# First chunk of attention's input moved ahead of bias and router work, experts' columns prepared earlier, last division in four pieces

## The chip, the core and the metric

The kernel runs on one core of a Trainium2 chip. The metric is the device time of one execution, in microseconds (us), as a median over several runs. TensorE (PE) does matrix products, VectorE (DVE) elementwise work and reductions, ScalarE (ACT) activations and copies, GpSimd (POOL) elementwise work and indirect transfers, and SyncE (SP) issues transfers. ACT and POOL issue transfers too. Each engine takes its own instructions in the order that was fixed when the program was built.

## The reference, cut to what matters

An image of 256 channels and 64 x 64 points passes through two layers. Layer 0 is a windowed linear attention on the image. Layer 1 takes the 4096 points as tokens of 256 channels: full attention with 8 heads, and then a mixture of 8 experts, of which each token uses two.

```python
x = x + _L0_conv_ref(_gn(x), L0_conv_Wq, L0_conv_Wk, L0_conv_Wv, L0_conv_Wout, L0_conv_bout)
t = _to_tokens(x)
t = t + _L1_attn_ref(_ln_t(t), L1_attn_w_qkv, L1_attn_b_qkv, L1_attn_w_out, L1_attn_b_out)
t = t + _L1_ffn_ref(_ln_t(t), L1_ffn_Wr, L1_ffn_br, L1_ffn_ln_g, L1_ffn_ln_b, L1_ffn_W1, L1_ffn_b1, L1_ffn_W2, L1_ffn_b2)
x = _from_tokens(t, x)
```

In attention, `qkv = x @ w_qkv + b_qkv`, a softmax over `q k^T / 16` for each head, and a projection with `w_out` and `b_out`. In the expert layer, `logits = xt @ Wr + br` choose two experts; each expert normalizes with its own gain and shift (`ln_g`, `ln_b`), multiplies by `W1`, adds `b1`, applies gelu, and multiplies by `W2`.

## The kernel before

All data is float32. The tokens lie as 32 tiles of 128 tokens (`t`, 264 columns: 256 channels and 8 columns for the router's logits). A chunk is four tiles, 512 tokens; there are 8 chunks (`NCH`).

**Layer 0** (to about 1000 us) runs twice, once for each half of the channels: `prepare` makes keys, values, queries and sums, and `attend` does the masked products. Its last sigmoids are those of `by_channel` (L367). `root` (L254) is a one-column tile whose square root serves only to have the table of sqrt loaded on ScalarE early; the square root of the group norm follows it.

**The q, k, v products of layer 1** (L814 to L965). First the transfers are issued: `w_out` on ACT's queue (L821), the QKV weights and the router's weights on SP's (L838, L839), the bias rows and two rows that are broadcast over all partitions on ACT's (L841 to L845). Then come two pieces of small work. The biases of q and k are transposed from six rows into six columns (`bqk`, L847 on TensorE, L849 on VectorE). The router's weights are folded into attention: the sums of their columns and the product with `b_out` (L856 on TensorE, L863 and L865 on VectorE), a transposed copy of `w_out` (L870, L871), and its product with the router's weights (L875, L882), so that the projection gives the logits' columns as well.

Then the loop over chunks. `begin(c)` takes the statistics of the chunk's four tiles (L793, L794 on VectorE), adds epsilon (L798, VectorE) and takes the square root (L799, ScalarE). It is called one chunk ahead. `end` takes the reciprocal (L802). For each tile, VectorE writes the normalized tile `hn` (L898, in two buffers), TensorE transposes it (L808), ScalarE copies it from PSUM to `act` (L809), and GpSimd adds the row of `b_out` to `t` (L908). Then q and k of the chunk are computed channel by channel (L914), and VectorE adds the bias (L918) and takes the largest absolute value (L919). The value products (L925) are evacuated by VectorE (L932), and the logits' part by ScalarE (L933). All these products, transposes included, share four PSUM banks. After the loop, a bound on the scores is computed (L950 to L965), and a branch (L978) on it chooses between two forms of attention; the first is taken, and the code of the other is jumped over at its end.

**Attention** (1120 to about 2287 us): for each chunk of queries and each half of the heads, scores (L1025), exp (L1036), sums of exp on VectorE (L1043) and products with the values (L991). The last sum is divided directly by `divide`: a reciprocal of 128 x 512 elements out of PSUM (L1072) and a product (L1067). Then the last four tiles are projected and added to `t` (L972, L975), with their statistics for the next norm (L793, L794).

**Routing and experts** (from about 2287 us). The experts' biases and norm parameters are loaded as three blocks of rows on ACT's queue (L1237), transposed on TensorE (L1239), copied on VectorE (L1240), and written to memory as one table, `crows` (L1244, ACT's queue), from which each slot of the expert loop later takes its expert's columns (L1216, SP's queue). Behind the first two of these copies on VectorE stand the norm of all tiles (L798, L799, L802) and the routing; it ends in lists by which GpSimd gathers tokens (L1445). The expert loop (L1485, L1494) runs to about 2829 us, and the image is put together at the end.

The order within each engine's queue comes from a planner that places instructions when the program is built, by their order in the source and by the times at which it expects inputs and buffers to be ready. A block under `tc.issue_after(ins)` keeps the instructions in it behind `ins` in the queue of the engine of `ins`.

## Time and profile before

| | us |
|---|---|
| median of 3 runs | 2881.29 (2879.69 to 2881.95) |
| the profiled execution, its own time | 2876.29 |
| its span, first to last instruction | 2874.5 |
| first q, k, v product (L914) starts | 1014.78 |
| first score product of attention (L1025) starts | 1120.05 |
| last division (L1072) starts | 2277.91 |
| norm ahead of routing (L798) starts | 2292.75 |
| first gather of an expert's tokens (L1445) starts | 2332.34 |

The times in the lower rows count from the span's start. In a timeline row, the first number is the start, the second the duration of what is merged in the row (as many instructions as xN says), then engine, line, operation, output<-inputs; in brackets stands how long the engine was idle before it and which work ended that idle time. "issue" there means that the engine waited for nothing that the profile shows. The granted clock is the share of TensorE's full clock.

### The profile page before, as it was taken

To read this page: it belongs to the slowest core of one execution; us is meant where nothing else is said; L and a number is where in the kernel's file an instruction comes from. 1 tells how busy PE (TensorE), PEld (TensorE's weight loads), DVE (VectorE), ACT (ScalarE), POOL (GpSimd) and SP (SyncE) were. 2 spreads that over 40 slices of the span, in tenths; PEclk is the share of its full clock that TensorE was granted. 3 is DMA by queue.
4 is the path that set the end of the run, shared out by engine and by line. 5 is a ranking of instruction groups with operands and counts; after the bars stand their busy time and mean duration, and the time that the engine had idled before them with its cause. 6 is when DMAs were issued, how large, how long until landed. Compare 5 with 4: busy or idle time off the path is not lost.

```text
span 2874.5 us, 73093 instructions
## 1 busy us (share of the span) xinstructions
PE 2722.7 (95%) x31182; PEld 1265.9 (44%) x31182; DVE 2078.1 (72%) x3019; ACT 1504.6 (52%) x2086; POOL 717.9 (25%) x804
## 2 busy tenths in 40 slices
PE   6889999988999999999999999999999779999996
PEld 5454346735434553222222222222222258888884
DVE  6758788575778777999999999999999841111113
ACT  3232423223332314888888888888888643222222
POOL 1067778116777621000000000000000022222220
PEclk9999999999999999999999999999999969999997
DMA  5000000000000000000000000000000056666665
GB/s 140 6 26 28 7 31 13 7 7 24 24 14 27 27 1 1 6 6 6 6 5 6 6 6 6 5 6 6 6 6 6 8 193 205 193 220 196 194 220 187
DMA packets 104212, 149.71 MB, mean 52 GB/s; under 512 B 18338, under 2 KB 79368, under 8 KB 103876
## 3 DMA queue, kind: packets, MB, share of 16 engines
q1 hardware_dynamic: 88984, 118.05, 12.7%
q0 software_dynamic: 6528, 17.83, 2.2%
q10 hardware_dynamic: 8364, 9.02, 0.9%
q8 instruction: 249, 4.08, 0.6%
q14 instruction: 87, 0.71, 0.1%
HBM read 126.76 MB, written 18.12 MB: 50 GB/s over the span
## 4 chain that ended last, share of the span: by engine, by line
PE 57%; DMA 2%; DVE 1%; issue 1%; ACT 0%; SPq 0%; POOL 0%; ACTq 0%; DVEq 0%; POOLq 0%
PE ps_two L1025 20%; PE ps_acc L991 18%; PE ps_hp L1485 8%; PE ps_yp L1494 8%; PE ps_den L972 1%; PE ps_den L991 1%; DMA y<-yrows 1%; PE ps_tp L1460 1%; DMA w<-in_L_ffn_W 0%; PE ps_two L972 0%; DVE t L1537 0%; DMA yrows<-y,target 0%; DVE rec L1072 0%; ACT pe L1036 0%; DVE total L1043 0%
## 5 line engine op out<-in xcount | busy, mean ns | idle before, releaser
L1036 ACT ACTIVATE pe<-ps_two 128x1024 f32<-128x1024 f32 x1024 | 992.4, 1021 | 142.5 <-PE ps_two L1025 127.3
L1043 DVE TENSOR_TENSOR total<-total,pe 128x1024 f32<-128x1024 f32 x928 | 1058.0, 1214 | 0.0
L1025 PE MATMUL ps_two<-qk 32*64 32x512 f32 x8192 | 620.2, 613 | 3.6 <-POOLq L978 1.8
L991 PE MATMUL ps_acc<-pe,v 128*32 128x512 f32 x4096 | 546.4, 605 | 0.2 <-ACT pe L1036 0.2
L561 ACT COPY sm<-ps_sc 128x384 f32<-128x384 f32 (+3 forms) x454 | 218.5, 511 | 523.8 <-PE ps_sc L734 344.3
L565 DVE TENSOR_TENSOR sm<-ps_sc,mask 128x512 f32<-128x512 f32 (+3 forms) x740 | 340.0, 519 | 71.8 <-PE ps_sc L734 68.0
L565 POOL TENSOR_TENSOR sm<-sm,mask 128x192 f32<-128x192 f32 (+3 forms) x428 | 350.1, 847 | 111.9 <-ACT sm L561 111.5
L1025 PEld LDWEIGHTS ps_two<-qk 32*64 32x64 f32 x8192 | 166.5, 129 | 421.0 <-PE ps_two L1025 379.0
L1488 ACT ACTIVATE hid<-ps_hp,cols 128x256 f32<-128x256 f32 (+1 forms) x288 | 133.0, 462 | 360.6 <-PE ps_hp L1485 359.5
L1303 POOL MEMSET on<- 128x256 f32 x1 | 0.3, 311 | 1166.6 <-PE ps_den L991 1166.6
L991 PEld LDWEIGHTS ps_acc<-pe,v 128*32 128x32 f32 x4096 | 80.7, 108 | 416.5 <-issue 402.5
L1485 PE MATMUL ps_hp<-xe,w 128*128 128x256 f32 (+1 forms) x1152 | 246.8, 371 | 0.0
L1494 PE MATMUL ps_yp<-w,hid 128*128 128x256 f32 x1088 | 240.8, 379 | 0.0
L734 PE MATMUL ps_sc<-qk 32*64 32x384 f32 (+3 forms) x3584 | 231.9, 458 | 0.0
L1485 PEld LDWEIGHTS ps_hp<-xe,w 128*128 128x128 f32 x1152 | 201.3, 190 | 39.5 <-ACT hid L1488 5.3
L1494 PEld LDWEIGHTS ps_yp<-w,hid 128*128 128x128 f32 x1088 | 204.2, 190 | 26.4
L750 PE MATMUL ps_acc<-sm,v 128*32 128x256 f32 (+3 forms) x2688 | 213.2, 419 | 0.2
L565 POOL TENSOR_TENSOR sm<-sm,ycut 128x384 f32<-128x384 f32 (+4 forms) x146 | 147.5, 1031 | 250.4 <-ACT sm L561 250.1
L1464 DVE TENSOR_SCALAR xe<-ps_tp,cols 128x256 f32<-128x256 f32 (+1 forms) x72 | 34.8, 525 | 239.6 <-PE ps_tp L1460 217.1
L565 DVE TENSOR_TENSOR sm<-ps_sc,ycut 128x384 f32<-128x384 f32 (+4 forms) x254 | 128.8, 559 | 90.0 <-PE ps_sc L662 88.0
L1496 DVE TENSOR_TENSOR y<-ps_yp,b 128x256 f32<-128x256 f32 x68 | 28.9, 424 | 194.8 <-PE ps_yp L1494 194.7
L734 PEld LDWEIGHTS ps_sc<-qk 32*64 32x64 f32 (+1 forms) x3584 | 108.6, 157 | 111.4 <-DVE sm L565 67.6
(237 smaller groups left out, 2230.6 us busy)
## 6 DMA issues: line engine op xcount, KB each, us to landing
w<-in_L_ffn_W SPq DMA_DIRECT2D x72, 1024.0 KB
by<-recs SPq DMA_DIRECT2D x48, 256.0 KB
b<-in_L_ffn_b SPq DMA_DIRECT2D x36, 128.0 KB
rows<-in_x SPq DMA_DIRECT2D x16, 256.0 KB
zrows<-act SPq DMA_DIRECT2D x4, 1024.0 KB
y<-yrows SPq DMA_DIRECT2D x8, 512.0 KB
y<-yrows ACTq DMA_DIRECT2D x8, 512.0 KB
rec<-recs SPq DMA_DIRECT2D x60, 64.0 KB
```

Of the source, the lines that this page charges most:

```text
L561: nc.scalar.copy(sm[:, :used], sc[:, :used])
L565: done = engine.tensor_mul(to, of, mk.unsqueeze(1).to_broadcast(list(to.shape)))
L734: nc.tensor.matmul(scs[h][u : u + rows, at : at + n], kT[hs[h], P * i + u : P * i + u + rows], qT[hs[h], CH * ix + CELL * c0 : CH * ix + C ...
L750: nc.tensor.matmul(acc[hs[h], CELL * c0 : CELL * c1], v[:, i, hs[h]], sms[h][:, at : at + n], start=not begun[0], stop=last and at == plac ...
L991: nc.tensor.matmul(to[D * hd : D * (hd + 1), :], lhsT(hd), rhs[:, hd, :], start=start, stop=stop, skip_group_check=True,)
L1025: nc.tensor.matmul(sc[hd // 2][CELL * u : CELL * (u + 1), hd % 2, :], qk[hs, 1, g, P * i + CELL * u : P * i + CELL * (u + 1)], qk[hs, 0, g ...
L1036: nc.scalar.activation(pe[:, pair, :], s, AF.Exp, scale=C**-0.5)
L1043: add = nc.vector.tensor_add(to, first[:, pair, :] if i == 1 else to, pe[:, pair, :])
L1464: nc.vector.tensor_scalar(xe[:, k, :n], tp[:, k, :n], cols[:, gain], cols[:, shift], op0=ALU.mult, op1=ALU.add,)
L1485: nc.tensor.matmul(hp[:, :n], w1[:, k, tok(m)], x_now[:, k, :n], start=k == 0, stop=k == KC - 1)
L1488: nc.scalar.activation(hid[:, m, :n], hp[:, :n], AF.Gelu, bias=cols[:, m : m + 1])
L1494: nc.tensor.matmul(yp, hid[:, m, tok(j)], w2[:, m, :], start=m == 0, stop=m == NH - 1)
```

## The change

- **First chunk.** The transposes of the biases and the router's work become two functions, `biases` and `router`. For chunk 0, normalization and transposes come first in the queues of VectorE and TensorE; behind them `biases` and the statistics of chunk 1; `router` follows chunk 0's value products on both engines. `hn` has four buffers.
- **Tables of sqrt.** One more square root of `root` stands behind the last sigmoid of layer 0, and `root` is kept through layer 0 for it; another, of one element, stands at the beginning of routing's code.
- **Experts' columns.** Loads, transposes and copies of the experts' rows move from the beginning of routing into the loop of the q, k, v products, after chunk 2. The copies go to ScalarE, the four transfers to SP's queue.
- **Last division.** Reciprocal and product are done in four pieces of 128 columns, in turn.

```diff
-            root = small.tile([P, 1], F32, name="root")
+            root = wts.tile([P, 1], F32, name="root")
             nc.scalar.sqrt(root, ident[:, :1])
...
+        sigmoid = [None]
...
-                nc.scalar.activation(qk[:, n, CH * i : CH * (i + 2)], pr.rearrange("p j n -> p (j n)"), AF.Sigmoid)
+                sigmoid[0] = nc.scalar.activation(qk[:, n, CH * i : CH * (i + 2)], pr.rearrange("p j n -> p (j n)"), AF.Sigmoid).ins
...
+            if g == KC - 1:
+
+                with tc.issue_after(sigmoid[0]):
+                    nc.scalar.sqrt(root, ident[:, :1])
             with tc.tile_pool(name="c_work", bufs=1) as work, psum("c_ps2", 1) as ps:
                 attend(g, work, ps, *of)
...
-            nc.tensor.transpose(tp[:, tok(k)], src[:, tok(k)], ident)
+            last = nc.tensor.transpose(tp[:, tok(k)], src[:, tok(k)], ident)
         nc.scalar.copy(dst, tp[:, :C].rearrange("p (k n) -> p k n", k=KC))
+        return last
...
+    e_dram = ctx.enter_context(tc.tile_pool(name="e_dram", bufs=1, space=bass.MemoryType.DRAM))
+    crows = e_dram.tile([NE, P, NH + 2 * KC], F32, name="crows")
+
+    def expert_columns(pool, ps):
+        cols = pool.tile([P, NE, NH + 2 * KC], F32, name="cols")
+        at = 0
+        for name, n in (("L1_ffn_b1", NH), ("L1_ffn_ln_g", KC), ("L1_ffn_ln_b", KC)):
+            rw = pool.tile([NE * n, P], F32, name=f"{name}_rows")
+            nc.sync.dma_start(rw, a[name].rearrange("e (k p) -> (e k) p", p=P))
+            tp = ps.tile([P, CH], F32, tag="mm", name="ps_mm")
+            nc.tensor.transpose(tp[:, : NE * n], rw, ident[: NE * n, : NE * n])
+            nc.scalar.copy(cols[:, :, at : at + n], tp[:, : NE * n].rearrange("p (e k) -> p e k", e=NE))
+            at += n
+        nc.sync.dma_start(crows.rearrange("e p n -> p e n"), cols)
...
-            tp = ps.tile([P, CH], F32, tag="mm", name="ps_mm")
-            nc.tensor.transpose(tp[:, :6], rows6, ident[:6, :6])
             bqk = win.tile([P, 6], F32, name="bqk")
-            nc.vector.tensor_copy(bqk, tp[:, :6])
...
-            rp = ps.tile([P, CH], F32, tag="mm", name="ps_mm")
...
+            def biases():
+                tp = ps.tile([P, CH], F32, tag="mm", name="ps_mm")
+                nc.tensor.transpose(tp[:, :6], rows6, ident[:6, :6])
+                nc.vector.tensor_copy(bqk, tp[:, :6])
+
+            def router():
+
+
+                rp = ps.tile([P, CH], F32, tag="mm", name="ps_mm")
+                for n, by in enumerate((lambda k: ones[:, :1], lambda k: bqk[:, 4 + k : 5 + k])):
+                    for k in range(KC):
+                        nc.tensor.matmul(
+                            rp[:, NE * n : NE * (n + 1)],
+                            by(k).to_broadcast([P, P]),
+                            wr[:, k, :],
+                            start=k == 0,
+                            stop=k == KC - 1,
+                        )
+                nc.vector.tensor_copy(wr_sum, rp[:, :NE])
+                nc.vector.tensor_copy(bo_wr, rp[:, NE : 2 * NE])
+                for j in range(KC):
+                    tp = ps.tile([P, CH], F32, tag="mm", name="ps_mm")
+                    for k in range(KC):
+                        nc.tensor.transpose(tp[:, tok(k)], wo[:, k, tok(j)], ident)
+                    nc.vector.tensor_copy(woT[:, j, :], tp[:, :C])
...
                 tp = ps.tile([P, CH], F32, tag="mm", name="ps_mm")
                 for k in range(KC):
+                    for j in range(KC):
+                        nc.tensor.matmul(
...
+                nc.vector.tensor_copy(wo[:, :, C:], tp[:, : KC * NE].rearrange("p (k e) -> p k e", e=NE))
...
             begin(0)
             for c in range(NCH):
-                if c + 1 < NCH:
+                if 0 < c < NCH - 1:
                     begin(c + 1)
                 norm.end(NB * c, NB * (c + 1))
                 for i in range(NB * c, NB * (c + 1)):
-                    hn = work.tile([P, C], F32, name="hn")
-                    nc.vector.tensor_scalar(
+                    hn = work.tile([P, C], F32, name="hn", bufs=4)
+                    last = nc.vector.tensor_scalar(
...
-                    to_channels(hn, act[:, :, tok(i)], ps)
+                    turned = to_channels(hn, act[:, :, tok(i)], ps)
 
                     nc.gpsimd.tensor_add(t[:, i, :C], t[:, i, :C], bo)
+                if c == 0:
+
+                    with tc.issue_after(last.ins), tc.issue_after(turned.ins):
+                        biases()
+                        begin(1)
                 for s in range(2):
...
-                    nc.vector.tensor_add(v[:, i, :], pv[:, :C], bv)
+                    biased = nc.vector.tensor_add(v[:, i, :], pv[:, :C], bv)
                     nc.scalar.copy(t[:, i, C:], pv[:, C : C + NE])
+                if c == 0:
+                    with tc.issue_after(biased.ins), tc.issue_after(product.ins):
+                        router()
+                if c == 2:
+                    expert_columns(win, ps)
...
-                                def divide(den=den, whole=whole, times=times):
+                                def divide(den=den, whole=whole, to=to):
                                     whole()
                                     rec = work.tile([P, CH], F32, tag="rec", name="rec")
-                                    nc.vector.reciprocal(rec, den[0])
-                                    times(rec)
+                                    for n in range(CH // P):
+                                        nc.vector.reciprocal(rec[:, tok(n)], den[0][:, tok(n)])
+                                        nc.vector.tensor_mul(to[:, tok(n)], to[:, tok(n)], rec[:, tok(n)])
...
+
+        root = small.tile([1, 1], F32, name="root")
+        nc.scalar.sqrt(root, ident[:1, :1])
         cst.update(constants_of("m", wts))
...
-        crows = dram.tile([NE, P, NH + 2 * KC], F32, name="crows")
         br = row_on_all("L1_ffn_br", NE, wts)
...
-            cols = r_work.tile([P, NE, NH + 2 * KC], F32, name="cols", bufs=1)
-            at = 0
-            for name, n in (("L1_ffn_b1", NH), ("L1_ffn_ln_g", KC), ("L1_ffn_ln_b", KC)):
-                rw = r_work.tile([NE * n, P], F32, tag="rw", name=f"{name}_rows")
-                nc.scalar.dma_start(rw, a[name].rearrange("e (k p) -> (e k) p", p=P))
-                tp = bank()
-                nc.tensor.transpose(tp[:, : NE * n], rw, ident[: NE * n, : NE * n])
-                nc.vector.tensor_copy(
-                    cols[:, :, at : at + n], tp[:, : NE * n].rearrange("p (e k) -> p e k", e=NE)
-                )
-                at += n
-            nc.scalar.dma_start(crows.rearrange("e p n -> p e n"), cols)
```

The lines of the biases' and router's former place, ahead of the loop, are removed; their text is that of the two functions.

## The prediction

> **What bounds the kernel now.** I read the page first, then the busy time by stretch around the start of layer 1 (about 1000 us), the timeline there, and the timeline at the end of layer 1's attention (2277 to 2296 us). The page gives the frame:

> ```profile
> span 2874.5 us, 73093 instructions
> PE 2722.7 (95%) x31182; PEld 1265.9 (44%) x31182; DVE 2078.1 (72%) x3019; ACT 1504.6 (52%) x2086; POOL 717.9 (25%) x804
> ...
> q8 instruction: 249, 4.08, 0.6%
> q14 instruction: 87, 0.71, 0.1%
> ```

> TensorE is busy 95% of the span, so time can only come out of the few stretches where it waits. The change touches two. The first, with the engines' busy time by stretch (PE, PEld, DVE, ACT, POOL, then granted clock, DMA share, GB/s):

> ```profile
> 1000.00:1007.00 7.00, 0.59 (x3) 0.19 (x1) 4.49 (x17) 1.49 (x2) 0.12 (x1) 0.72 0.64 190
> 1007.00:1015.00 8.00, 7.01 (x30) 5.85 (x31) 5.50 (x26) 1.81 (x6) 2.90 (x4) 0.50 0.00 0
> 1015.00:1028.00 13.00, 13.00 (x33) 6.95 (x34) 9.69 (x31) 0.68 (x5) 1.51 (x2) 0.80 0.00 1
> 1028.00:1041.00 13.00, 11.90 (x42) 6.94 (x41) 12.94 (x46) 2.57 (x12) 3.02 (x4) 1.00 0.01 1
> ...
> 1054.00:1067.00 13.00, 12.05 (x45) 7.08 (x42) 9.31 (x17) 1.91 (x8) 2.98 (x4) 1.00 0.00 0
> ```

> For 6.4 us TensorE does nothing while weights land (190 GB/s, all of it before 1007); then 7 us of small work at half clock; then products, which fill TensorE (12 of 13 us per chunk) until attention starts at 1120. The timeline shows what each engine waited for:

> ```profile
> 1003.38 1.28 ACT L799 ACT_TABLE_LOAD   x1 [8.06 <-DVE ln_mv L794]
> ...
> 1007.26 0.24 PE L847 MATMUL ps_mm<-cst,bias_rows 6*128 6x6 f32 x1 [6.67 <-DMA L_attn_b_out_all<-in_L_attn_b_out]
> ...
> 1007.61 0.17 DVE L849 COPY bqk<-ps_mm 128x6 f32<-128x6 f32 x1 [2.95 <-PE ps_mm L847]
> ...
> 1009.50 0.40 DVE L898 TENSOR_SCALAR hn<-t,ln_mv,ln_rstd 128x256 f32<-128x256 f32 x1
> ...
> 1014.78 9.81 PE L914 MATMUL ps_mm<-act,wqkv 128*128 128x512 f32 x16 [0.46 <-ACT act L809]
> ```

> VectorE's queue is in order: the bias copy (L849) waits, through L847, for the bias rows' DMA until 1007.6 (the row names the last of the DMAs behind it), and the first chunk's normalization (L898), whose statistics were ready by 1003.3, stands behind it. So the first product starts at 1014.78. The second place is the end of attention:

> ```profile
> 2277.91 3.36 DVE L1072 RECIPROCAL rec<-ps_den 128x512 f32<-128x512 f32 x1 [1.15 <-PE ps_den L991]
> 2281.37 0.69 DVE L1067 TENSOR_TENSOR act<-act,rec 128x512 f32<-128x512 f32 x1
> ...
> 2289.93 0.17 DVE L1315 TENSOR_SCALAR steps<-cstm 128x16 f32<-128x16 f32 x1 [2.66 <-issue]
> 2292.52 0.31 DVE L1240 COPY cols<-ps_mm 128x64 f32<-128x64 f32 x2 [2.42 <-issue]
> 2292.75 0.17 DVE L798 TENSOR_SCALAR ln_rstd<-ln_mv 128x32 f32<-128x32 f32 x1
> ```

> Here everything hangs on VectorE: last division, projection's sums, then (after the branch around the other attention) routing, up to the gathers at 2332.

> **First chunk ahead.** Statistics of four tiles end about 1003.1 (chunk 1's no longer mixed in). The sqrt then runs without the 1.28 us table load, at 1003.3; reciprocal 0.17, four normalizations at about 0.37 apart from 1003.7 to 1005.3; eight transposes at half clock (four took 1.09 us) and the ScalarE copies (0.37 each) end about 1006.9. The bias transpose, now behind them on TensorE, still waits for its rows until 1007.2; the QKV weights, on SP's queue, are in by then, since the DMA share is 0.00 after 1007. The first product starts at about 1007.5, not 1014.78: **7.3 us** earlier. Behind the waiting bias copy on VectorE are now chunk 1's statistics (4 x 0.5 us), which are not wanted before 1020. GpSimd's sums L908, now early, wait for the b_out row; only the projection, much later, needs them. The DMA issues on ACT's queue stay where they were and end at 1003.07, before the sqrt.

> The moved router work is not gone. It is 16 small matmul instructions and 4 transposes, 5.0 us before at half clock (1.02 + 1.00 + 1.09 + 1.89), in time when TensorE had nothing else ready. Now it stands between chunk 0's and chunk 1's products at full clock: 16 x 0.215 us (the value products[...] are 3.72/16 = 0.23 apart) + 4 x 0.15 = 4.0 us. A chunk's boundary has 1.0 us of idle TensorE that could hide some, and the waits for VectorE's woT copies may add as much; I take **4.0** (3 to 6).

> [...] The row: the clock read 0.50 from 1004 to 1020, through 7 us of small matmuls, and rose only 5.3 us after the dense products began. [...] by the row the same 5.3 us. I take the row, and ±0.9 us[...].

> **Table loads.** The new sqrt after the last sigmoid of layer 0 costs 1.28 + 0.2 us of ScalarE, hidden by its 17 us without work there (611.5 to 630.4, but for one copy). If placed before that copy, 0.2 us. The second, ahead of routing, replaces a load at 2288.5 that nothing waited for: nothing.

> **Four hn buffers.** With two, each chunk's tiles 2 and 3 are normalized only after the transposes of 0 and 1, and TensorE waits 0.49 and 0.46 us at each boundary. With four, one wait remains (the last value bank's ScalarE copy). About 0.25 us over 6 or 7 boundaries: **1.5** (0 to 3.5).

> **Experts' columns.** Added in chunk 2: three row loads and one store on SP (about 0.4 us of issue each; the store waits there for the copies, and nothing of SP's stands behind it before attention; the loads are 48 KB among 1.3 MB, about 0.15 us of transfer), three transposes (0.2 us each) and three ScalarE copies. They take three PSUM banks out of the rotation of four: **-0.5** (0 to -1.5). Taken away at the end: two VectorE copies ahead of L798, 0.23 us, with their semaphore instructions about **0.3**; four ACT issues, which hid behind VectorE anyway. The third copy lay in a ScalarE wait: nothing.

> **Last division in pieces.** Reciprocals of 128x128 take 0.94 us at L620, from SBUF; a quarter of L1072 is 0.84; I take 0.9. Each piece has a 0.1 us dependency and a product of 0.29 (L1319's shape): 5.2 us instead of 4.15, but the first projection starts after 1.3. VectorE then need not wait: 5.2 plus 3.3 us of sums and statistics end at 2286.4, not 2287.26: **0.9** (0.5 to 1.2).

> **After the branch.** VectorE stands idle 2.66 us, runs one instruction, and stands again (2.42), with no wait on another engine. In this stretch the instruction queue q14 brings two blocks. [...] The row has 0.71 MB in 87 packets, about 8 KB each[...]. The branch target lies just ahead of a block's end, so two fetches are paid. The pieces add at least six instructions ahead of it; the target should slide into the next block, and one fetch falls away. [...] Semaphore instructions can shift it too, so I take most: **1.9** (0 to 2.25).

> **Sum.** 7.3 - 4.0 + 1.5 - 0.5 + 0.3 + 0.9 + 1.9 = 7.4 us. Against the profiled execution: span 2874.5 to 2867.1, its own time 2876.3 to 2868.9. The median of the runs lies 5.0 us above that execution; the same difference gives 2881.3 - 7.4 = **2873.9**. A measurement tells about 0.2% (5.8 us) from no change, so the forecast lies only just outside.

> **Rivals.**
> - *Both fetches stay*: the target is still ahead of a block's end. For it: the semaphore count is unknown. 7.4 - 1.9 = 5.5: 2875.8, within 0.2%. Chance 0.15.
> - *VectorE sets the pace in the first chunks.* It was 12.94 of 13 us busy from 1028 to 1041. A chunk needs 9.35 us of it; with 28 tiles' statistics (14 us) and the router's 1.4 over three chunks that is 43.4 against 38.6: up to 4.8 us lost, 2878.7. Against it: statistics have no haste. Chance 0.10.
> - *It doesn't do what it says*: the products wait for the QKV weights to 1011, which nothing used before 1014. 3.5 us lost, 2877.4. Against: no DMA after 1007. Chance 0.05.
> - *More*: boundaries and router hide fully (+2 and +1): 2870.9. Chance 0.15.
> - *Slower*: the router on TensorE waits for two woT copies in VectorE's full queue, with chunk 1's products queued behind. [...] It must eat 7.4 + 5.8 = 13.2 us, so it decides from two waits of 5.3 us; then 2887. Against: these copies kept TensorE 0.1 us before. Chance 0.05.

> The likeliest has 0.50, its own range 2871.5 to 2876. The bound of 0.2% lies at 2875.5: **faster 0.70** (0.48 of the likeliest, 0.15 of the fourth, about half of the first rival), **same 0.25** (the rest of these two, and the second and third rivals), **slower 0.05**. The range, 2870 to 2879, leaves out the slower case and the tails.

> **What would show it.** First L914 near 1007.5, L799 without a table load, attention at about 1115.8 (1120.05 less 4.3); one idle gap on VectorE after the branch; L798 near 2285.4 (2292.75 less 7.4). Wrong if L914 starts after 1010, if TensorE pauses over 2 us before chunk 1, or if the gap is still double.

## The result and the profile after

In a first series, six runs of each kernel, the changed kernel took 2869.84 us (2867.64 to 2871.2) and the kernel before 2880.08 (2879.19 to 2881.95): ratio 0.9962, 95% interval 0.995 to 0.9975. A second series gave 2863.21 against 2877.4, ratio 0.9954 (0.994 to 0.9967). The change makes the kernel faster by 0.25 to 0.6%. The forecast, 7.4 us or a ratio of 0.9974, lies at the edge of the first interval and outside the second: right in sign, too small by 3 to 7 us. 2869.84 is also 0.16 us below the range's low end.

The head and two queues of the changed kernel's page:

```profile
span 2869.0 us, 73086 instructions
PE 2723.5 (95%) x31182; PEld 1263.6 (44%) x31182; DVE 2079.2 (72%) x3022; ACT 1505.2 (52%) x2091; POOL 718.0 (25%) x804
...
q8 instruction: 249, 4.08, 0.6%
q14 instruction: 87, 0.71, 0.1%
```

Its own time is 2870.81 us. Nothing in the totals tells the story: TensorE's work is the same, and so are the page's two instruction queues (q8, q14). The stretches tell it. The busy time by stretch at the start of layer 1, whose first load is now issued at 1004.04 (before: 1000.63), same columns as before:

```profile
1004.00:1007.00 3.00, 0.01 (x1) 0.00 (x0) 2.61 (x10) 0.18 (x1) 0.12 (x1) 0.96 0.55 112
1007.00:1011.00 4.00, 2.04 (x9) 1.67 (x9) 3.09 (x11) 1.51 (x5) 0.00 (x0) 0.50 0.74 258
1011.00:1016.00 5.00, 5.00 (x7) 2.23 (x8) 4.82 (x18) 0.41 (x2) 4.47 (x7) 0.50 0.01 2
1016.00:1024.50 8.50, 8.50 (x27) 5.09 (x26) 8.06 (x22) 0.50 (x3) 1.30 (x2) 0.94 0.00 1
1024.50:1028.80 4.30, 3.39 (x30) 2.91 (x28) 3.20 (x13) 1.56 (x6) 1.04 (x2) 1.00 0.00 0
1028.80:1041.00 12.20, 11.78 (x40) 6.91 (x40) 12.20 (x40) 2.17 (x10) 2.50 (x4) 1.00 0.01 2
```

The seven microseconds of small work at half clock are gone from the front (row two holds chunk 0's own eight transposes and, at its end, that of the biases). They come back, shorter, in row five, between chunk 0 and chunk 1 at full clock. In the timeline of the same place:

```profile
1006.82 0.20 ACT L805 ACTIVATE ln_rstd<-ln_rstd 128x4 f32<-128x4 f32 x1 [8.08 <-DVE ln_rstd L804]
...
1007.34 1.38 DVE L924 TENSOR_SCALAR hn<-t,ln_mv,ln_rstd 128x256 f32<-128x256 f32 x4
...
1010.90 0.24 PE L875 MATMUL ps_mm<-cst,bias_rows 6*128 6x6 f32 x1 [1.11 <-DMA bias_rows<-in_L_attn_b_out]
...
1011.12 10.01 PE L945 MATMUL ps_mm<-act,wqkv 128*128 128x512 f32 x16
...
1024.53 0.51 PE L884 MATMUL ps_mm<-wqkv,ones 128*128 128x8 f32 x4
...
1024.89 0.59 PE L884 MATMUL ps_mm<-wqkv,bqk 128*128 128x8 f32 x4
...
1025.34 0.64 PE L896 MATMUL ps_mm<-cst,wo 128*128 128x128 f32 x4
...
1026.37 0.36 PE L901 MATMUL ps_mm<-wqkv,woT 128*128 128x8 f32 x2 [0.39 <-DVE woT L897]
...
1027.05 0.73 PE L901 MATMUL ps_mm<-wqkv,woT 128*128 128x8 f32 x6
```

No table load stands before the square root (L805). The four normalizations follow each other (L924). TensorE then waits 1.11 us for the bias rows (L875), and the first product (L945) starts 7.08 us after the first load; it was 14.15. The end of attention, VectorE's timeline:

```profile
2277.06 1.77 DVE L1109 RECIPROCAL rec<-ps_den 128x128 f32<-128x128 f32 x2 [1.18 <-PE ps_den L1027]
2278.75 0.42 DVE L1110 TENSOR_TENSOR act<-act,rec 128x128 f32<-128x128 f32 x2
2279.09 1.76 DVE L1109 RECIPROCAL rec<-ps_den 128x128 f32<-128x128 f32 x2
2280.77 0.42 DVE L1110 TENSOR_TENSOR act<-act,rec 128x128 f32<-128x128 f32 x2
2281.11 0.77 DVE L1011 TENSOR_TENSOR t<-ps_two,t 128x264 f32<-128x264 f32 x2
...
2286.87 0.17 DVE L1340 TENSOR_SCALAR steps<-cstm 128x16 f32<-128x16 f32 x1 [2.66 <-issue]
2286.96 0.17 DVE L804 TENSOR_SCALAR ln_rstd<-ln_mv 128x32 f32<-128x32 f32 x1
...
2289.26 0.43 DVE L1303 TENSOR_TENSOR logit<-logit,L_ffn_br_all 128x256 f32<-128x256 f32 x1 [0.65 <-DVE again L1278]
```

The pieces end when the whole division would have (2281.11 is 4.05 us after its start; before, 3.36 + 0.69), but the projection's sums follow without a pause. After the branch the first idle gap is as long as before (2.66). The second, 2.42 before, has shrunk to 0.65 and moved behind six more instructions.

Single executions differ by several microseconds ahead of layer 1 (its first load is issued anywhere from 998.0 to 1004.4 us in the fourteen profiles of this case), so runs are compared by stretch, each counted from the start of the event that opens it to the start of the one that ends it (last statistics: their end).

| us | before | after | after, again |
|---|---|---|---|
| first load to first product | 14.15 | 7.08 | 6.90 |
| chunk 0, first product to first value product | 9.65 | 9.85 | 9.00 |
| last value product of chunk 0 to chunk 1 | 2.65 | 4.48 | 4.49 |
| the same, chunk 2 to 3 (experts' columns) | 2.51 | 2.62 | 2.62 |
| the same, other chunks | 2.51 to 2.58 | 1.97 | 1.96 |
| first load to start of attention | 119.42 | 111.70 | 110.67 |
| attention to its last division | 1157.86 | 1161.32 | 1157.79 |
| last division to last statistics | 9.36 | 7.15 | 7.15 |
| last statistics to first gather | 45.07 | 43.24 | 43.23 |

The edited stretches gain 7.7 + 2.2 + 1.8 = 11.8 us in the first profile (12.8 in the second). The first span is only 5.5 us shorter because two things went the other way: layer 0 took 3.4 us more, and attention 3.5 more through the clock (last section). Layer 0 has one small edit, the added square root at 614 us; but TensorE's 8000th product there, at about 546 us, was 2.0 us late already, so most of the 3.4 us does not come from it.

### The profile page after: what moved, and what is told of

It is laid out like the page before. It is cut to its first block, busy times and chain, and to the rows that moved or that the text cites. A ratio compares the mean times of both kernels' runs of the same rounds, so it can differ in the third digit from the quotient of the medians.

```text
span 2869.0 us, 73086 instructions
## 1 busy us (share of the span) xinstructions
PE 2723.5 (95%) x31182; PEld 1263.6 (44%) x31182; DVE 2079.2 (72%) x3022; ACT 1505.2 (52%) x2091; POOL 718.0 (25%) x804
## 3 DMA queue, kind: packets, MB, share of 16 engines
q8 instruction: 249, 4.08, 0.6%
## 4 chain that ended last, share of the span: by engine, by line
PE 57%; DMA 1%; DVE 1%; issue 1%; SPq 0%; ACT 0%; POOL 0%; POOLq 0%; DVEq 0%; ACTq 0%
PE ps_two L1061 20%; PE ps_acc L1027 18%; PE ps_hp L1510 8%; PE ps_yp L1519 8%; PE ps_den L1008 1%; PE ps_den L1027 1%; DMA y<-yrows 1%; PE ps_tp L1485 0%; DMA w<-in_L_ffn_W 0%; DVE t L1562 0%; DMA xs<-zrows,source 0%; PE ps_mm L1568 0%; DMA yrows<-y,target 0%; DVE rec L1109 0%; POOL xs L1470 0%
## 5 line engine op out<-in xcount | busy, mean ns | idle before, releaser
L1072 ACT ACTIVATE pe<-ps_two 128x1024 f32<-128x1024 f32 x1024 | 992.6, 1021 | 145.0 <-PE ps_two L1061 130.2
```

Source lines behind the costliest of these rows:

```text
L1072: nc.scalar.activation(pe[:, pair, :], s, AF.Exp, scale=C**-0.5)
```

## The experiments

**Two hn buffers in the changed kernel**

```
-  hn = work.tile([P, C], F32, name="hn", bufs=4)
+  hn = work.tile([P, C], F32, name="hn", bufs=2)
```

> The changed kernel with two hn buffers instead of four. Theory (the buffers take away TensorE's waits at each chunk's boundary): the chunks' products start 12.8 us apart again instead of 12.28, so attention starts 3.2 to 3.8 us later after the first weights' transfer than the changed kernel's 111.7 us. Rival (the closer chunks come from elsewhere, such as the new order of VectorE's queue): still 12.28, attention at 111.7. On the fetch after the branch: the program then has 14 more VectorE instructions ahead of the branch's target, which puts the target behind a block's boundary; theory: one idle gap of about 2.7 us and none of 0.65 after it.

Measured: 2872.76 us (one run; before 2881.27). Between the later chunks TensorE again takes 2.51 us, with the experts' columns 3.12; the seven boundaries together are 4.0 longer than the changed kernel's. Attention starts 115.83 after the first load, 4.1 later; that this agrees is partly chance, since chunk 1 lost 1.7 us to the half clock here, while the first product and chunk 0 were 1.5 quicker. The second gap after the branch is gone. So by the boundaries the buffers are worth 4.0 us. That is more than the 1.5 of the prediction, and above its upper bound of 3.5.

**Four hn buffers in the kernel before, and nothing else**

```
-  hn = work.tile([P, C], F32, name="hn")
+  hn = work.tile([P, C], F32, name="hn", bufs=4)
```

> The kernel before with four hn buffers and nothing else. Theory of the buffers: 12.28 us from chunk to chunk where the kernel before has 12.82, from chunk 1 on, so attention starts about 116.2 us after layer 1's first load instead of 119.4 (3.2 sooner). Theory that the changed kernel's closer chunks came from something else (statistics begun in another order, the router moved): 12.82 stays, and attention starts at 119.4. Theory of the blocks: the branch's target then stands 16 VectorE instructions ahead of the block's end (it was 2), so the first stop after the branch stays at 2.7 to 3.0 us, and the second, 2.13 before, is gone. Median by both theories 5.3 us below the kernel before; by the first alone 3.2.

Measured: 2870.47 us (2868.51 to 2871.51) against 2878.43, ratio 0.9968 (0.9954 to 0.9981): 8.0 us by the medians, where 5.3 were expected. Last statistics to first gather takes 42.97 (2.1 less). Attention starts at 114.51 (expected 116.2), 4.9 sooner than before: 4.0 from the boundaries, the rest in the first product and in chunk 0's clock. So one word of the change brings 4.0 us at the boundaries and, by way of the second gap after the branch (below), 2.1 behind it; the other 0.9 lies in stretches that also vary between profiles of one kernel. A chunk boundary of the kernel before, TensorE's timeline:

```profile
1053.84 0.60 PE L808 MATMUL ps_mm<-cst,hn 128*128 128x128 f32 x4
1054.93 0.73 PE L808 MATMUL ps_mm<-cst,hn 128*128 128x128 f32 x4 [0.49 <-DVE hn L898]
1056.13 7.13 PE L914 MATMUL ps_mm<-act,wqkv 128*128 128x512 f32 x16 [0.46 <-ACT act L809]
```

and one with four buffers:

```profile
1064.89 1.28 PE L808 MATMUL ps_mm<-cst,hn 128*128 128x128 f32 x8
1066.64 1.55 PE L914 MATMUL ps_mm<-act,wqkv 128*128 128x512 f32 x3 [0.46 <-ACT act L809]
```

The wait of 0.49 for tiles 2 and 3 goes whole, and the transposes run 0.05 closer; the wait of 0.46 for ScalarE's copy stays whole. Over the seven boundaries that is 0.68 + 0.60 + 5 x 0.54 = 4.0 us.

**The router's products behind the biases, ahead of chunk 0's own products**

```
   biases()
+  router()
   begin(1)
...
-  if c == 0:
-      with tc.issue_after(biased.ins), tc.issue_after(product.ins):
-          router()
```

> The changed kernel with the router's work right behind the biases, ahead of chunk 0's products. Theory (the work itself is cheap at full clock and partly fits into the boundary's idle time; at half clock it stands alone on TensorE): the first product starts 4 to 5 us later than the changed kernel's 7.1 us after the first transfer, the boundary before chunk 1 shrinks by 2.0 to 2.4 us, and attention starts 2 to 3 us later. Rival (moving the router behind chunk 0 wins nothing, only the order of the first chunk did): attention starts within 0.5 us of the changed kernel's 111.7 us.

Measured: 2868.68 us (one run). First product 10.26 after the first load (3.2 later, expected 4 to 5). The boundary shrinks from 4.48 to 1.97: the router costs **2.51** there, not 4.0. But the first chunk's products took 11.65 (9.85), as the half clock lasted longer, and the boundary with the experts' columns took 0.4 more; attention starts 2.9 later. Without the clock's 1.8, the router's place between the chunks is worth about 1 us; how much of the 1.8 is chance one run can't say.

**The last division whole again**

```
-  for n in range(CH // P):
-      nc.vector.reciprocal(rec[:, tok(n)], den[0][:, tok(n)])
-      nc.vector.tensor_mul(to[:, tok(n)], to[:, tok(n)], rec[:, tok(n)])
+  nc.vector.reciprocal(rec, den[0])
+  nc.vector.tensor_mul(to, to, rec)
```

> The changed kernel with the last reciprocal and product undivided. Theory: from the start of the reciprocal to the last tile's statistics 9.3 us again instead of 7.15, TensorE's projection starting 4.2 us after the reciprocal instead of 2.0. Rival (the pieces gain only because the statistics after them are ordered better): 7.2 to 8. After the branch, 14 VectorE instructions stand ahead of the block's end; they take over 2.3 us, so by the fetch theory there is one gap of about 2.7 us and no second one.

Measured: 2867.9 us (one run). Division to last statistics 9.82, against 7.15 in pieces: 2.7 us. VectorE's timeline shows where:

```profile
2272.17 3.36 DVE L1108 RECIPROCAL rec<-ps_den 128x512 f32<-128x512 f32 x1 [1.18 <-PE ps_den L1027]
2275.98 0.69 DVE L1109 TENSOR_TENSOR act<-act,rec 128x512 f32<-128x512 f32 x1 [0.46 <-DVE rec L1108]
2277.48 0.99 DVE L1011 TENSOR_TENSOR t<-ps_two,t 128x264 f32<-128x264 f32 x2 [0.81 <-PE ps_two L1008]
```

VectorE waits 0.46 for its own reciprocal and 0.81 for the projection; ahead of the last sum it waits another 1.06. In pieces none of these appears. The kernel before didn't have the first of them (its product started 0.10 after the reciprocal's end), so this run overstates the gain: the change itself brought the 2.2 of the table.

**Where the branch's target stands.** Two runs move only the number of VectorE instructions ahead of the target. In the kernel before, and in the changed one:

```
+  junk = wts.tile([P, 1], F32, name="junk")
+  for _ in range(3):    # 6 in the changed kernel
+      nc.vector.memset(junk, 0.0)
```

> The kernel before with three one-element memsets on VectorE at the very beginning, while it waits for the image. Theory (the second gap after the branch is the fetch of the next block of instructions, which ended two instructions behind the branch's target): the target now stands behind the boundary, the gap of 2.4 us ahead of the experts' columns is gone, and the first copy of columns starts within 0.5 us of the first instruction after the branch. Rival (the gap was a wait of the columns' copies for released memory or for another engine): it stays at 2.2 to 2.4 us.

Measured: 2875.59 us (one run; before 2881.27). The second gap is gone, last statistics to first gather 43.15 (45.07): 1.9 us, though the first gap is 0.3 longer here (2.97).

> The changed kernel with six one-element memsets on VectorE at the very beginning, while it waits for the image. This moves the branch's target back to where it stood before the change, two instructions ahead of a block's end. Theory (fetch of the next block): after the branch two instructions run, then a second gap of 2.1 to 2.3 us stands where the changed kernel has 0.6, and routing is 1.5 to 1.7 us later. Rival (the gap of before belonged to the experts' columns, which are gone here): the second gap stays at 0.6 or vanishes.

Measured: 2868.05 us (one run; before 2877.4). The second gap is back, as in the kernel before, and the first gather comes 1.4 us later. VectorE's timeline with six instructions added:

```profile
2282.70 0.17 DVE L1343 TENSOR_SCALAR steps<-cstm 128x16 f32<-128x16 f32 x1 [2.67 <-issue]
2282.78 0.17 DVE L807 TENSOR_SCALAR ln_rstd<-ln_mv 128x32 f32<-128x32 f32 x1
2285.04 0.42 DVE L1303 TENSOR_TENSOR logit<-ln_mv,wr_sum 128x256 f32<-128x256 f32 x1 [2.08 <-issue]
```

The VectorE instructions of each program ahead of the target, counted in the compiled program (a jumped-over form of attention included), against the second gap:

```
program                      ahead   runs before the 2nd gap   2nd gap, us
four buffers, before          7089   -                         none
whole division                7091   -                         none
changed kernel                7097   8                         0.58
router early                  7098   7                         0.76
kernel before; after + 6      7103   2                         2.13; 2.08
kernel before + 3             7106   -                         none
two buffers, after            7111   -                         none
```

One place, behind instruction 7105, fits all of them: with two instructions left to it the second gap is 2.08 to 2.13 us, with seven and eight 0.76 and 0.58, with 14 or 16, or past it, there is none. In the kernel before and in the changed one, single packets of 8 KB start on q14, by the page an instruction queue, at 1.0 and at 3.4 us after the branch. The first stop ends 2.83 us after the branch in both; the second ends 5.14 and 5.15 us after it, whether two instructions ran ahead of it or eight. Each stop ends 1.72 to 1.82 us after the start of one of these packets. That the packets are fetches of the instructions that follow, and that one ends behind 7105, is the author's reading of these times and counts. (The gaps here are from the end of any instruction, semaphores too, so 0.58 for the row's 0.65 and 2.13 for its 2.42.)

**The changed kernel again**, unchanged, five runs.

> The changed kernel unaltered, for its time beside the following kernels and for a second trace. Theory [...]: times fall into groups 3 to 3.5 us apart, and this trace may show the clock either way; the stretches outside such drops repeat to 0.3 us (last division to last statistics 7.15, the second gap after the branch 0.58 to 0.65, chunks 12.28 apart). Rival (the drop belongs to the changed program): the clock reads 0.50 for 8 us after the start of attention here too.

Measured: 2863.21 us (2862.32 to 2866.35) against 2877.4; the table above has its stretches. Every edited stretch repeats within 0.2 us, except chunk 0's products. Attention takes 1157.79, as before the change, so its longer time in the first profile doesn't belong to the changed program as such. Six of the fourteen profiles met a half clock near attention's start, among them one with the old order (three instructions added to the kernel before: 1159.77); how often each kernel meets it, fourteen profiles can't say. The times do fall into two groups, 2862.3 to 2863.2 and 2865.9 to 2866.4, but drops at attention's start don't explain them: the profiled execution is of the upper group and had none.

**A guard against a stop at the start of attention**: the exp's table loaded early, and one filler product behind the bound's.

```
+  early = small.tile([1, 1], F32, name="early")
+  with tc.issue_after(logits.ins):
+      nc.scalar.activation(early, ident[:1, :1], AF.Exp)
...
+  fill = ps.tile([P, CH], F32, tag="mm", name="ps_mm")
+  with tc.issue_after(bounding.ins):
+      for k in range(KC):
+          nc.tensor.matmul(fill, wqkv[:, k, tok(0)], act[:, k, chunk(0)], ...)
```

> The changed kernel with two things at the start of attention: a one-element exp on ScalarE behind the last copy of the logits, so that exp's table is loaded during the branch, and one more product (4 matmul instructions, 1.7 us, into a bank that nobody reads) behind the bound, so that TensorE doesn't pause. Theory [...]: the first exp runs 1.3 us sooner after the first score products, the clock stays at 1.00, and the median is 1.3 us plus some part of 3.4 us below the changed kernel's, 1.5 to 4 us. Rival [...]: 1.3 us or less.

Measured: 2862.39 us (2861.11 to 2865.12), ratio 0.9951 (0.9937 to 0.9965), not to be told from the changed kernel's 2863.21. In the profiled execution, attention to division took 1156.53, 1.3 less, at full clock; but chunk 1 ran a while at half clock (its dense products 8.67 us, not 6.97), which took 1.7 back.

**The early table alone** (the edit above without the filler)

> The changed kernel with a one-element exp behind the last of the logits' copies, so that the exp's table is loaded while TensorE still works on the last products. Theory that attention's first step waits for the table: start of attention to last division 1156.5 us at a steady clock (1157.8 without), 1.3 less. Theory that the earlier run's 1.3 came from its filler product[...]: 1157.8 stays, or 1161.3 where the clock drops.

Measured: 2865.88 us (one run), attention to division 1157.38. By itself that is inconclusive: the clock was halved for 3.41 us from 0.21 us after attention's start. But the next run had the same drop, 3.41 us from 0.11, without the early table, and took 1158.54. Like against like, the table brings 1.16 us.

**w_out's load behind the bias rows, alone**

```
-  nc.scalar.dma_start(wo[:, :, :C], a["L1_attn_w_out"]...)   # first on ScalarE's queue
   ... bias rows, b_out on all rows, bv ...
+  nc.scalar.dma_start(wo[:, :, :C], a["L1_attn_w_out"]...)   # last
```

> The changed kernel with one DMA issue moved: w_out's 256 KB are issued on ScalarE's queue behind the bias rows and the broadcast rows, not ahead of them. Theory that the first product waits for the bias rows, and these for w_out on the same queue: first product about 3.6 us after layer 1's first load (6.9 to 7.1 without the move), everything behind it up to the start of attention 3.3 sooner (about 107.5 after the first load), median about 3 us below the changed kernel's 2863 to 2870. Rival, that the table load ahead or the filler in the earlier run brought it: 6.9 stays and the median does not move. Second rival: the router, which needs w_out, then holds chunk 1 up, and chunk 0 to chunk 1 takes 3 us more than 16.9.

Measured: 2865.62 us (2862.72 to 2866.76) against 2878.43, ratio 0.9951 (0.9936 to 0.9967): no different from the changed kernel. The 3 us that were expected from the median did not show. The expected 3.6 for the first product was misread: the first load that it counts from was w_out's, which the edit itself moves 2.0 us back. Counted from the QKV weights' issue, which stays, the first product comes at 5.50, not 7.05 (first profile) or 6.87 (second). That is 1.4 to 1.6 sooner, and the bias transpose no longer waits for its DMA. The router then stands 0.4 us longer (4.86), and in this execution chunk 1 met the half clock (8.63 for 6.97): attention starts at 110.71, where the changed kernel had 110.64 and 111.67.

**w_out's load last and the early table, with the target moved past the place behind 7105** (10 added instructions), with the filler and then without (12 added):

> The changed kernel with the two additions at the start of attention, ten one-element memsets on VectorE at the very beginning (so that the branch's target lies behind a block's boundary), and the transfer of w_out moved behind the bias rows and broadcast rows on ACT's queue. Theory: 1.3 us and some of 3.4 as before, 0.6 us for the second gap after the branch, and 0.3 to 1.1 us for a first product that waits less for the bias rows: 3 to 6 us below the changed kernel. Rival (the QKV weights land no sooner than the bias rows did): the first product stays at 7.1 us after the first transfer and the gain is 2 to 4.

Measured: **2860.06 us** (2859.29 to 2861.42), ratio 0.9942 (0.9928 to 0.9955), 3.2 us below the changed kernel's 2863.21. The first product comes 5.61 after the weights' issue (1.3 sooner), attention takes 1156.56 (1.2 less), and no second gap is left.

> The changed kernel with three additions: w_out's issue behind the bias rows, the exp's table loaded ahead, and twelve one-column instructions at VectorE's start that put the branch's target past a block's end. It is the earlier run's best version without its filler product. Theory that the filler product cost more (1.7 us in the last chunks) than it brought: 84.6 us from chunk 1 to the last value product, first product 3.6 after the first load, no second stop after the branch, median 2858 to 2860. Rival, that the filler's clock guard was worth its cost: the granted clock drops to 0.50 at the start of attention in some executions, each 3.4 us longer, and the median is 2860 to 2862 with a wider spread.

Measured: 2862.08 us (2860.62 to 2867.91), ratio 0.9944 (0.9931 to 0.9958) against 2878.43. Attention to division is 1156.58 at full clock without the filler, so the early table gives the 1.2 without it. In this profile chunk 1 lost 1.1 to the clock. The two versions can't be told apart by their ratios; that the filler costs 1.7, which the expectation assumed, is refuted, since with it chunk 1 to the last value product was 84.62, as in the changed kernel.

## Why the prediction was right or wrong

The paths were read rightly in the main. The forecast failed by the size of three terms, the buffers (1.5 forecast, 4.0 measured), the router (4.0 against 2.5) and the division (0.9 against 2.2), and by the direction in which the branch's target moves.

**First chunk ahead: right.** Forecast 7.3, measured 7.07. The bias copy was what held VectorE, and with it behind the normalizations the first product waits for the bias rows' DMA alone, as the prediction had it. What the earlier table load adds was not measured apart. ScalarE's last copy ended 0.92 us ahead of the first product, so a load of 1.28 us would have held it up by some 0.4 us (an estimate from these two).

**The signs that the prediction named** were mostly absolute times, and layer 0 ended 3.4 us later in this execution. The first product started at 1011.12, past the 1010 that was to mean "wrong", but 7.08 us after the first load; attention started at 1115.74, next to the 1115.8 that was named, but 3.5 us sooner after the first load than that meant. The one failure and the one agreement both come from layer 0's end, not from the edits. The sign that held is the gap: it is still double.

**The router between the chunks: place right, size wrong.** Forecast 4.0 (3 to 6), measured 2.51, below its range. The step that failed is "16 x 0.215": the eight-column products took 0.51, 0.59, 0.36 and 0.73 us for 4, 4, 2 and 6, mostly 0.12 to 0.15 each. The value products from which 0.215 was taken have weight loads of the same shape and the same 0.19 us each, but 264 columns, and were 0.23 apart (3.72/16): the loads alone didn't set that pace. Its own rows had the better figure: the same work at half clock, 5.0 us, is 2.5 at full clock, and 2.83 were measured, part of them in the boundary's idle time. The wait for VectorE's woT copy was 0.39 us.

**Four hn buffers: the largest miss.** Forecast 1.5 (0 to 3.5), measured 4.0. The waits were read rightly, 0.49 and 0.46, and that one of the two would remain. The step that failed is "about 0.25 us over 6 or 7 boundaries": the row it rested on says 0.49, and no reason is given for halving it. The run with four buffers alone shows the wait gone whole, 0.54 per boundary and more at the first two.

**Experts' columns:** forecast -0.5, measured -0.65 (2.62 against 1.97). Their row loads don't come in chunk 2, as the prediction had it: SP's queue is free, and the first is issued 0.94 us after the QKV weights, among the loads that chunk 0 waits for. What that costs was not tested. **Copies ahead of L798:** forecast 0.3, measured 0.4 (last statistics to first gather, with two instructions left ahead of the second gap in both: 45.07 before, 44.65 with six added to the changed kernel).

**Division in pieces:** forecast 0.9 (0.5 to 1.2), measured 2.2. The pieces cost 4.05 and not 5.2: products of 0.21, not 0.29, and no dependency of 0.1 (the rows come in pairs of independent pieces). The 3.3 behind them were 3.1.

**"One fetch falls away": wrong direction, and the size near it by luck.** Forecast 1.9, measured 1.4. The prediction let "at least six instructions" slide the target *into the next block*. The target moved six the other way, from 7103 to 7097: four hn buffers need 14 fewer instructions, the division adds six, and two come from elsewhere. Both of q14's packets remain, at 1.0 and 3.4 us after the branch; eight instructions now run ahead of the second stop, where two did. The first stop is as long in both kernels (2.66 us). How many instructions a packet of 8 KB holds was not shown: all counts lie around one place.

**Sum.** By measured terms: 7.1 - 2.5 + 4.0 - 0.65 - 0.2 (chunk 0's clock) + 0.4 + 2.2 + 1.4 = 11.75, the stretches' 11.8. The forecast's 7.4 fell short by 2.5 (buffers), 1.5 (router) and 1.3 (division), less half a microsecond of the second gap. The medians, 10.2 and 14.2 us lower, lie about this.

**The rivals.** "More" (boundaries and router hide: 2870.9) was the nearest and named two of the three missing terms. VectorE as pace-setter falls: it was busy 12.20 of 12.20 us in chunk 1, as the row above shows, and chunk 2's products still came 12.28 us after chunk 1's, no later than with the other chunks. Late QKV weights and the long waits for woT didn't occur. That both fetches stay was true by q14's two packets, and yet 1.4 us of the second gap's 2.1 were saved.

**The clock: right, just about in its bounds.** Chunk 0's products took 9.85 and 9.00 us, where the row's half clock meant 9.65; both lie within the ±0.9 that was allowed around it. Four more profiles with the same first chunk have 8.58 to 9.97, so the bounds were a little narrow. The row's 5.3 us of dense products at half clock doesn't hold as a constant: the two profiles have 5.9 and 4.1. The last section has the lengths of the half clock.

## What to carry to other kernels

When a row names a wait and an edit takes away its cause, count the whole wait at every place it occurs, and only then look for what hides it: two more buffers in one pool brought 4.0 us at the boundaries, nearly as much as the whole reordering of the first chunk (7.1 less the router's 2.5). Take the spacing of small matmuls from matmuls of their own shape. Where an engine stops after a branch with nothing to wait for, count its instructions up to the target: semaphores count too (one of the two ahead of the second gap in the kernel before is one), and three short ones decided 1.9 us here.

## What the runs showed of the hardware

```profile
1007.14:1010.55 3.41, 2.25 (x11) 1.86 (x11) 2.13 (x10) 0.84 (x3) 1.24 (x2) 0.50 0.28 87
1010.55:1013.97 3.42, 3.06 (x11) 2.22 (x10) 1.70 (x8) 0.20 (x1) 1.53 (x3) 0.50 0.00 0
1013.97:1017.38 3.41, 3.41 (x9) 1.95 (x8) 1.04 (x6) 0.00 (x0) 0.48 (x1) 0.50 0.00 0
1017.38:1020.79 3.41, 3.41 (x5) 1.35 (x4) 1.73 (x4) 0.00 (x0) 0.97 (x2) 0.50 0.00 0
1020.79:1024.20 3.41, 3.41 (x9) 1.52 (x8) 3.17 (x7) 0.20 (x1) 1.02 (x2) 1.00 0.00 0
```

Behind stretches that TensorE filled to 66 and 89%, mostly with small products, the clock stayed at half (in the kernel before even behind one at 97%, from 1009.97 to 1013.38), and so it did behind the full one from 1013.97, a third of which went to six eight-column products. In the last version, without the filler, it rose behind one at 92%:

```profile
1003.41:1006.83 3.42, 0.38 (x3) 0.31 (x4) 3.00 (x14) 0.20 (x1) 0.00 (x0) 1.00 0.78 251
1006.83:1010.24 3.41, 3.15 (x10) 1.90 (x10) 3.41 (x18) 1.70 (x5) 1.94 (x3) 0.50 0.47 153
1010.24:1013.66 3.42, 3.42 (x9) 1.52 (x8) 3.42 (x10) 0.20 (x1) 2.87 (x5) 1.00 0.00 0
```

Nor did TensorE have to stand still for a drop: in the run with w_out's load last, the clock was halved at 1025.09 behind a stretch with 2.29 of 3.39 us busy. What decides stays open. In the run with the guard, a piece of half clock in chunk 1's dense products cost 1.7 us (8.67 for 6.97), so how many of them an execution meets moves its time by microseconds. The changed kernel's first profile met three from 1116 on, at the start of attention:

```profile
1116.00:1119.40 3.40, 3.26 (x24) 0.65 (x8) 0.00 (x0) 1.58 (x2) 0.00 (x0) 0.50 0.00 0
1119.40:1122.80 3.40, 2.62 (x12) 0.50 (x16) 0.66 (x1) 3.10 (x4) 0.00 (x0) 0.50 0.00 0
1122.80:1126.20 3.40, 3.40 (x28) 0.53 (x24) 1.74 (x2) 0.62 (x2) 0.00 (x0) 0.50 0.00 0
1126.20:1129.60 3.40, 3.40 (x40) 0.84 (x40) 2.49 (x3) 3.17 (x4) 0.00 (x0) 1.00 0.00 0
```

The second profile of the same kernel met none, and attention was 3.5 us shorter. That is over half of what made a gain of 12 us show as 5.5 in one pair of spans.

**Small loads behind a large one on the same queue.** The bias rows, issued behind w_out's 256 KB, let the bias transpose run only 6.8 us after the QKV weights' issue; issued ahead of it, they let it run at 5.0, with no wait for a DMA. Their own issue came 0.75 us sooner by that; the rest is their landing. Whether the order in the queue or the 256 KB in flight held them, no run here tells apart.
